# Moving the scratch writes of v from SyncE's queue to ScalarE's, with a new plan, in an RWKV block

## The chip, the cores and the metric

The kernel runs on one core of one Trainium2 chip. The metric is device time in microseconds of one execution; the time before is the median of 3 runs.

## The reference

One RWKV layer over 8 batches of 256 tokens and 512 channels, in float32, with 32 heads of 16. Cut to what matters:

```
xn = layernorm(x);  sx = shift(xn) - xn
five mixes x5[g] = xn + sx * (maa[g] + tanh((xn + sx*maa_x) @ maa_w1)[g] @ maa_w2[g])
w = exp(-exp(time_decay + tanh(x5[1] @ decay_w1) @ decay_w2))
k, v, r = x5[0] @ Wk.T, x5[2] @ Wv.T, x5[3] @ Wr.T;   g = silu(x5[4] @ Wg.T)

for each token t, per head:            # s is a 16x16 state, kept over t
    a = k_t (outer) v_t
    out_t = r_t @ (u * a + s)
    s = a + w_t * s

x = x + (groupnorm(out) * g) @ Wo.T    # time mixing
x = x + sigmoid(xr @ Wfr.T) * (square(relu(xk @ Wfk.T)) @ Wfv.T)   # xr, xk: mixes of layernorm(x)
```

The state of each head and each of its 16x16 entries is a recurrence over 256 tokens.

## The kernel before

Each batch goes through three stages. `inputs_of_scan` loads x, normalizes and transposes it (channels on partitions), makes the five mixes and projects k, v, r, g and the decay. `scan` runs the recurrence. `rest` does the group norm, the output projection Wo, and the feed-forward part with the weights fk, fr and fv, which are streamed from memory again for each batch. The stages of three batches in a row overlap: while batch b is scanned, batch b+1 is projected and batch b-1 finished.

The scan works on four blocks of 128 channels (8 heads) per batch. Partitions hold the 16 key entries of 8 heads; the value entries are spread over four steps of four. Every partition needs v of its own head, so v must be copied to other partitions. This is done through scratch tiles in memory, called vo: v of a block is written to vo (128 KB, L665), and for each of the four steps a transfer reads 32 rows of vo, repeated over the partitions, into an SBUF tile vs (512 KB, L685). ScalarE puts the state at the start into the first column of vs (L687), VectorE multiplies it with k (`kv`, L690) and runs the recurrence (`tensor_tensor_scan`, L692), GpSimd multiplies by r (L695), and TensorE adds up over the keys (`gather`, L703).

v comes out of PSUM by a ScalarE copy in `projected` (L642); one copy holds two blocks. There are 4 vo tiles, 4 vs tiles, 3 tiles of v and 3 PSUM tiles `ps` for projections. TensorE does the projections in pieces of four matmuls, by `project` (L538) and `project_tokens` (L553).

All transfers, 32 vo writes and 128 vs reads among them, are made by the helper `dma` and issued by SyncE (L366), in one queue in order.

The order of all work is set by a planner, `Plan`, that runs when the kernel is built. `Plan.add` records each operation with its engine, an estimated duration and the buffers it reads and writes. `Plan.order` then plays the work through: it keeps a time for each engine and picks the operation with the smallest sum of its earliest start and `PULL` times its rank. The ranks are the long list of integers `AIMS`, one for each operation of each stage of each batch. After an operation on another engine, one waits for `LATENCY` more:

```
    LATENCY = {"PE": 0.25, "DVE": 0.12, "ACT": 0.2, "POOL": 0.15, "DMA": 2.6}
    ...
                same = o.engine == op.engine
                o.ready = max(o.ready, op.end + (0.03 if same else self.LATENCY[op.engine]))
```

All transfers are of the engine "DMA" to the planner, so in the plan of before a vs read may follow the vo write that it needs by 0.03 us. In the running kernel it waits on a semaphore until the write has landed, and SyncE's queue with it. The order that comes out is the order of the instructions in each engine's queue.

Of the kernel before, what the change touches and what calls it, by code (L numbers as in the profile page):

```python
# [13 lines left out]
NB, T, E = 8, 256, 512  # L14
# [42 lines left out]
class Plan:  # L57
# [21 lines left out]
    def add(self, engine, us, outs, ins, emit, mode=None, into=()):  # L79
        op = Op(engine, us, outs, ins, emit, mode)  # L80


        op.bufs += [b for b in into if b not in op.bufs]
        edges = set()
        for b in ins:
            edges.add(b.writer)
            b.readers.append(op)
        for b in outs:
            edges.add(b.writer)
            edges.update(b.readers)  # L90
            b.writer, b.readers = op, []
        for o in edges - {None, op}:
            op.before.append(o)
            o.after.append(op)
        self.stages[-1].append(op)

    def stage(self):
# [116 lines left out]
    """  # L214
    PULL = 0.01

    def sequence(self, phases):
        self.ops = []
# [666 lines left out]
```

## Time and profile before

| what | value |
|---|---|
| median of 3 runs | 763.6 us (762.99 to 765.69) |
| profiled execution | 770.98 us, span 769.2 us |
| mean granted TensorE clock | 0.968 |
| TensorE busy | 692.6 us (90%) |
| VectorE busy | 596.7 us (78%) |
| GpSimd busy | 558.0 us (73%) |
| ScalarE busy | 345.6 us (45%) |
| moved by the transfers | 124.47 MB, mean 162 GB/s |
| hardware queue of SyncE | 123.84 MB, 59.4% of 16 engines' span |

In the profile's rows the engines are PE (TensorE), DVE (VectorE), ACT (ScalarE), POOL (GpSimd) and SP (SyncE); SPq is SyncE's queue of instructions, whose transfers aren't counted as busy time. A row of waits reads "who <- whom: us in total, times, longest us". The chain is the work that ended last, followed back to what released each step; its shares are of the span. A row of a stretch gives its length and, for each engine, busy time and the number of instructions, then the granted clock, the busy share of the 16 DMA engines and GB/s. A row of a transfer gives KB each and the median us from issue to landing.

### The profile page before, as it was taken

The numbers are of one execution on the slowest core, as the hardware profiler recorded it, in microseconds if no ns is written. First come the engines' busy times: TensorE is split into PE (matmuls) and PEld (weight loads), VectorE is DVE, ScalarE is ACT, GpSimd is POOL, SyncE is SP. The second block draws the span as 40 slices with busy tenths as digits, with TensorE's granted clock in tenths as the row PEclk, the third lists the DMA queues.
The fourth block names the chain that finished last, engine by engine and source line by source line (L and its number), as shares of the span: only waits on it lengthen the run. The fifth ranks groups of instructions, "written<-read, shape, count | busy, mean of one in ns | idle before, by whom it ended". The sixth has DMA issues, their size and how long they took to land.

```text
span 769.2 us, 10151 instructions
## 1 busy us (share of the span) xinstructions
PE 692.6 (90%) x3616; PEld 457.3 (59%) x3616; DVE 596.7 (78%) x612; ACT 345.6 (45%) x672; POOL 558.0 (73%) x462
## 2 busy tenths in 40 slices
PE   4897797999889998999989998999988998998987
PEld 3585465667555566657655675656755475644553
DVE  1437897999989985998689997979688988899120
ACT  4342432514673325742476334654365244534441
POOL 3546685679988777987679778788686875978351
PEclk9799799999979999999999999999998999999999
DMA  8857345364665648753759547863577628774632
GB/s 270 284 123 191 78 116 147 101 157 119 176 171 122 162 117 214 213 154 100 184 139 260 130 119 184 222 187 111 127 180 219 150 91 189 214 202 133 196 136 82
DMA packets 53889, 124.47 MB, mean 162 GB/s; under 512 B 6928, under 2 KB 12432, under 8 KB 53840
## 3 DMA queue, kind: packets, MB, share of 16 engines
q1 hardware_dynamic: 53840, 123.84, 59.4%
q8 instruction: 28, 0.46, 0.3%
q14 instruction: 21, 0.17, 0.1%
HBM read 115.43 MB, written 8.39 MB: 161 GB/s over the span
## 4 chain that ended last, share of the span: by engine, by line
PE 30%; DMA 10%; DVE 10%; issue 2%; ACT 2%; POOL 2%; SPq 1%; POOLq 0%; DVEq 0%; ACTq 0%
PE ps L553 11%; PE ps L538 9%; DMA vs<-vo 7%; DVE st L692 5%; DVE kv L690 4%; DMA vo<-v 3%; PE pat L703 2%; PE ps L592 2%; PE ps L569 2%; PE ps L612 1%; PE pat L675 1%; PE ps L738 1%; POOL mix L525 1%; SPq L366 1%; DVE mix L601 1%
## 5 line engine op out<-in xcount | busy, mean ns | idle before, releaser
L695 POOL TENSOR_TENSOR st<-st,r 128x1024 f32<-128x1024 f32 x128 | 301.5, 2357 | 79.7 <-DVE st L692 77.0
L692 DVE TENSOR_TENSOR_SCAN st<-wrep,kv 128x1024 f32<-128x1024 f32 x128 | 292.1, 2282 | 15.3 <-PE pat L703 4.4
L690 DVE TENSOR_TENSOR kv<-vs,kp 128x1024 f32<-128x1024 f32 x128 | 156.7, 1224 | 54.1 <-ACT vs L687 47.4
L687 ACT ACTIVATE vs<-s,cm 128x4 f32<-128x4 f32 x128 | 38.1, 299 | 189.4 <-DMA vs<-vo 177.1
L553 PE MATMUL ps<-Ws,mix 128*128 128x512 f32 x256 | 117.1, 598 | 6.0 <-ACT r L642 2.0
L603 POOL TENSOR_TENSOR mix<-mix,xn 128x512 f32<-128x512 f32 x80 | 86.3, 1091 | 16.1 <-DVE mix L601 15.9
L601 DVE SCALAR_TENSOR_TENSOR mix<-ps,vec,sx 128x256 f32<-128x256 f32 x160 | 67.7, 475 | 19.0 <-PE ps L592 18.5
L553 PEld LDWEIGHTS ps<-Ws,mix 128*128 128x128 f32 x256 | 47.2, 190 | 59.3 <-issue 46.5
L703 PE MATMUL pat<-st,con 128*32 128x256 f32 x1024 | 72.5, 407 | 6.0 <-POOL st L695 5.2
L538 PE MATMUL ps<-mix,Wg 128*128 128x256 f32 x256 | 62.9, 397 | 10.8 <-ACT ta L576 4.7
L538 PE MATMUL ps<-mix,Ws 128*128 128x256 f32 x256 | 60.9, 387 | 4.3 <-POOL mix L525 2.6
L538 PEld LDWEIGHTS ps<-mix,Wg 128*128 128x128 f32 x256 | 49.4, 197 | 23.5 <-ACT ta L576 5.1
L538 PE MATMUL ps<-mix,Wr 128*128 128x256 f32 x256 | 60.5, 384 | 2.2 <-ACT v L642 1.8
L553 PE MATMUL ps<-Ws,g 128*128 128x512 f32 x128 | 58.9, 599 | 2.1 <-POOL g L750 1.1
L538 PE MATMUL ps<-mix,Wv 128*128 128x256 f32 x256 | 58.7, 383 | 2.3 <-POOL mix L603 1.1
L538 PE MATMUL ps<-mix,Wk 128*128 128x256 f32 x256 | 59.5, 383 | 1.2 <-ACT r L642 0.9
L538 PEld LDWEIGHTS ps<-mix,Ws 128*128 128x128 f32 x256 | 48.0, 192 | 16.8 <-POOL mix L525 5.0
L703 PEld LDWEIGHTS pat<-st,con 128*32 128x32 f32 x1024 | 32.6, 115 | 40.6 <-issue 14.2
L525 POOL TENSOR_TENSOR mix<-mix,xn 128x512 f32<-128x512 f32 x48 | 52.1, 1092 | 5.9 <-ACT mix L523 5.9
L538 PEld LDWEIGHTS ps<-mix,Wk 128*128 128x128 f32 x256 | 47.9, 190 | 13.0 <-issue 4.0
L538 PEld LDWEIGHTS ps<-mix,Wv 128*128 128x128 f32 x256 | 47.7, 190 | 12.9 <-POOL mix L603 2.7
L538 PEld LDWEIGHTS ps<-mix,Wr 128*128 128x128 f32 x256 | 48.0, 192 | 11.5 <-ACT v L642 2.8
(77 smaller groups left out, 867.2 us busy)
## 6 DMA issues: line engine op xcount, KB each, us to landing
vs<-vo SPq DMA_DIRECT2D x128, 512.0 KB, 4.8
Ws<-in_fk SPq DMA_DIRECT2D x32, 256.0 KB, 4.3
Ws<-in_wo SPq DMA_DIRECT2D x32, 256.0 KB, 4.6
Ws<-in_fr SPq DMA_DIRECT2D x32, 256.0 KB, 4.2
Ws<-in_fv SPq DMA_DIRECT2D x32, 256.0 KB, 4.4
xt<-in_x SPq DMA_DIRECT2D x16, 256.0 KB, 4.8
x<-in_x SPq DMA_DIRECT2D x16, 256.0 KB, 4.8
vo<-v SPq DMA_DIRECT2D x32, 128.0 KB, 4.8
```

What stands on the lines that cost most here:

```text
L525: gp(512, t, [t, xn[q]], lambda q=q, t=t: nc.gpsimd.tensor_tensor(t(), t(), xn[q]()[:, :, 1 : T + 1], ALU.add), 1.8)
L538: nc.tensor.matmul(ps()[:, m, :], lhsT=w[k]()[:, o : o + P], rhs=src[k // 2]()[:, k % 2, :], start=(k == 0), stop=(k == NK - 1),)
L553: nc.tensor.matmul(ps().rearrange("p m t -> p (m t)"), lhsT=src[h]()[:, k % 2, n * P : (n + 1) * P], rhs=w[k](), start=(k == 0), stop=(k = ...
L569: nc.tensor.matmul(px()[:, i, :], lhsT=w1()[:, k, i * P : (i + 1) * P], rhs=xin[k // 2]()[:, k % 2, :], start=(k == 0), stop=(k == NK - 1),)
L592: nc.tensor.matmul(ps[g, q]()[:, m, :], lhsT=w2()[lo : lo + MAA, k * P : (k + 1) * P], rhs=ta()[lo : lo + MAA, i, :], start=True, stop=True,)
L601: dve(256, [t], [p_, vec, sx[q]], lambda g=g, q=q, m=m, t=t, p_=p_: nc.vector.scalar_tensor_tensor(t()[:, m, :], p_()[:, m, :], col(f"maa_ ...
L603: gp(512, t, [t, xn[q]], lambda q=q, t=t: nc.gpsimd.tensor_tensor(t(), t(), xn[q]()[:, :, 1 : T + 1], ALU.add), 1.8)
L687: act(4, vs, [s0, cm], lambda i=i, blk=blk, vs=vs: nc.scalar.activation(vs()[:, :, 0:1], s0()[:, blk, 4 * i : 4 * i + 4].rearrange("p (n o ...
L690: dve(4 * T, [kv], [vs, kp], lambda m=m, vs=vs, kv=kv, kp=kp: nc.vector.tensor_tensor(kv(), vs(), kp()[:, m : m + 1, :].to_broadcast([P, 4 ...
L692: dve(4 * T, [st], [w, kv], lambda w=w, kv=kv, st=st: nc.vector.tensor_tensor_scan(st().rearrange("p n t -> p (n t)"), w().rearrange("p n ...
L695: gp(4 * T, st, [st, r], lambda m=m, st=st, r=r: nc.gpsimd.tensor_tensor(st(), st(), r()[:, m : m + 1, :].to_broadcast([P, 4, T]), ALU.mult))
L703: nc.tensor.matmul(pat()[32 * i : 32 * i + 32, 0, :], lhsT=con()[:, s : s + 32], rhs=done[i]()[:, j, :], start=(j == 0), stop=(j == 3),)
```

## The change

The vo write is taken from the helper `dma` and issued by ScalarE (`nc.scalar.dma_start`), which puts it on ScalarE's own hardware queue. To the planner it is an operation of ScalarE of 0.5 us whose result is there 0.2 + 1.9 = 2.1 us after its end: `add` takes a `lag` for that, each operation carries its own `op.lag`, and the short 0.03 us between two operations of one engine holds only for those with a lag under 1, so no longer for a transfer that reads what another one wrote. All the integers of `AIMS` and `PULL` are replaced. What is computed, the tiles and the buffers stay.

```
-    def add(self, engine, us, outs, ins, emit, mode=None, into=()):
+    def add(self, engine, us, outs, ins, emit, mode=None, into=(), lag=0.0):
         op = Op(engine, us, outs, ins, emit, mode)
+        op.lag = self.LATENCY[engine] + lag
...
     AIMS = """
-        -664 -111 -501 -184 -363 -1421 -163 -60 -19 -194 201 188 -323 -12 166 -419 -366 -388 11 112 -1280
...
+        1 24 -4 17 28 45 31 38 50 16 11 52 46 38 60 67 62 63 36 47 17 51 -41 75 -17 3 7 -7 -3 20 29 56 51
...
-    PULL = 0.01
+    PULL = 0.0607
...
-                b.until = max(b.until, op.end + self.LATENCY[op.engine])
+                b.until = max(b.until, op.end + op.lag)
...
-                same = o.engine == op.engine
-                o.ready = max(o.ready, op.end + (0.03 if same else self.LATENCY[op.engine]))
+                same = o.engine == op.engine and op.lag < 1
+                o.ready = max(o.ready, op.end + (0.03 if same else op.lag))
...
             vo = new("vo", f"vo{b}_{blk}")
-            dma(vo, lambda m=m, v=v: v()[:, m, 0:T], vo, 128, v)
+            plan.add("ACT", 0.5, [vo], [v], lambda m=m, v=v, vo=vo: nc.scalar.dma_start(
+                out=vo(), in_=v()[:, m, 0:T]), lag=1.9)
```

216 rows, old and new, of the table AIMS are left out of this document.

## The prediction

> **What bounds the kernel now.** I read the page first (busy shares, chain, groups), then the waits of the two in-order queues that the change touches, then the stretch from one batch's scan to the next.
>
> ```profile
> span 769.2 us, 10151 instructions
> PE 692.6 (90%) x3616; PEld 457.3 (59%) x3616; DVE 596.7 (78%) x612; ACT 345.6 (45%) x672; POOL 558.0 (73%) x462
> ...
> PE 30%; DMA 10%; DVE 10%; issue 2%; ACT 2%; POOL 2%; SPq 1%; POOLq 0%; DVEq 0%; ACTq 0%
> PE ps L553 11%; PE ps L538 9%; DMA vs<-vo 7%; DVE st L692 5%; DVE kv L690 4%; DMA vo<-v 3%; PE pat L703 2%; PE ps L592 2%; PE ps L569 2%; PE ps L612 1%; PE pat L675 1%; PE ps L738 1%; POOL mix L525 1%; SPq L366 1%; DVE mix L601 1%
> ```
>
> TensorE is the fullest engine and has the largest part of the chain, so time is won where TensorE stands idle, and at most that much: 769.2 - 692.6 = 76.6 us. The second thing on the chain is the way of v through memory: 7% for the reads (vs from vo) and 3% for the writes (vo from v), the only part of the chain that the change names.
>
> Stretches from the first vo write of each batch to that of the next (the first eight rows; the eighth ends with the last scan, the ninth is the tail) show how full each engine is there:
>
> ```profile
> core 0: us, PE busy (x) PEld busy (x) DVE busy (x) ACT busy (x) POOL busy (x), PEclk, DMA share, GB/s
> 44.68:114.96 70.28, 60.36 (x321) 44.16 (x323) 54.41 (x53) 25.60 (x54) 45.80 (x33) 0.90 0.56 139
> 114.96:185.65 70.69, 62.99 (x374) 44.47 (x367) 64.02 (x69) 23.00 (x46) 50.27 (x36) 0.98 0.50 127
> 185.65:282.07 96.42, 88.50 (x474) 56.57 (x474) 89.65 (x84) 44.09 (x87) 78.08 (x58) 0.95 0.57 154
> 282.07:365.67 83.60, 79.13 (x433) 53.93 (x432) 69.89 (x76) 41.58 (x80) 67.94 (x62) 0.98 0.64 164
> 365.67:453.86 88.19, 82.78 (x457) 55.74 (x457) 75.80 (x75) 46.78 (x90) 70.14 (x51) 1.00 0.63 168
> 453.86:542.68 88.82, 84.24 (x455) 55.70 (x455) 77.01 (x82) 47.32 (x92) 72.94 (x64) 1.00 0.63 166
> 542.68:629.85 87.17, 80.38 (x428) 52.78 (x427) 73.50 (x71) 39.48 (x76) 67.22 (x50) 0.96 0.63 164
> 629.85:709.30 79.45, 72.04 (x365) 43.33 (x364) 69.21 (x59) 38.21 (x75) 60.53 (x43) 1.00 0.66 179
> 709.30:769.20 59.90, 52.85 (x195) 28.34 (x194) 10.77 (x17) 20.19 (x36) 22.71 (x23) 0.99 0.42 140
> sum 724.52, PE 663.28 PEld 435.03 DVE 584.26 ACT 326.26 POOL 535.63; mean PE 73.70 PEld 48.34 DVE 64.92 ACT 36.25 POOL 59.51
> ```
>
> Stretch less PE busy is TensorE's idle time: 9.9, 7.7, 7.9, 4.5, 5.4, 4.6, 6.8 and 7.4 us in the eight stretches, 54.2 together, and 7.1 in the tail. Even the tail has TensorE 88% busy, with work of the batch before still in it. So an idle microsecond saved in the eight stretches should come off the end nearly one for one.
>
> Now the queue of SyncE, which issues every transfer in order, and the engines behind it:
>
> ```profile
> SPq L366 <- DVE kv L690: 215.0, 74, 7.5
> SPq L366 <- DMA vo<-v: 75.7, 19, 9.0
> SPq L366 <- PE ps L553: 64.6, 33, 11.0
> SPq L366 <- ACT v L642: 59.7, 11, 12.6
> SPq L366 <- DMA vs<-vo: 50.6, 17, 6.4
> ```
> ```profile
> ACT vs L687 <- DMA vs<-vo: 177.1, 81, 8.4
> ...
> DVE kv L690 <- ACT vs L687: 47.4, 19, 11.8
> ```
>
> 215.0 us of SyncE's waiting is harmless: it waits for a vs tile to come free. 59.7 us is waiting for v to be computed before a vo write, and 75.7 us for a vo write to land before its first vs read; all other transfers queue behind. ScalarE's column write into vs (L687) then waits 177.1 us for the reads, and VectorE 47.4 us for that write. The start of a batch, here the last one, looks like this on SyncE's queue:
>
> ```profile
> 629.85 0.33 SPq L366 DMA_DIRECT2D vo<-v  x1
> 631.63 2.45 SPq L366 DMA_DIRECT2D vs<-vo  x4
> 634.41 0.33 SPq L366 DMA_DIRECT2D vo<-v  x1
> 643.86 1.16 SPq L366 DMA_DIRECT2D vs<-vo  x2
> 645.11 0.54 SPq L366 DMA_DIRECT2D vo<-v  x1
> ```
> ```profile
> vs<-vo SPq DMA_DIRECT2D x128, 512.0 KB, 4.8
> ...
> vo<-v SPq DMA_DIRECT2D x32, 128.0 KB, 4.8
> ```
> ```profile
> 629.85 1.70 DMA vo<-v
> 634.41 9.30 DMA vo<-v
> ```
>
> The first write lands in 1.70 us, with nothing before it. The second is issued behind four reads of 512 KB and takes 9.30 us for 128 KB, and the reads of its block go out at 643.86, just after. A small write stands behind large reads; this is what a queue of its own takes away.
>
> **The change, part by part.** (1) 32 vo writes leave SyncE's queue for ScalarE's. On SyncE one takes 0.33 (the rows above) to 0.59 us; I take 0.43, so 32 x 0.43 = 13.7 us more on ScalarE, whose 345.6 us busy become some 359 of 769. I cost it at nothing: its cover is ScalarE's 423 us of idle time; if that cover is gone it costs up to 13.7. The bound below is zero, as the instruction does no work there that another removes.
>
> (2) A write's waits move with it. v is made by ScalarE's own copy (L642), so the 59.7 us of SyncE standing for v go, and the weights, x rows and reads behind it are issued earlier. The other wait comes along: a vo buffer (four of them) must have been read by its four vs reads of the batch before. Behind a ScalarE that waits stand the copies out of PSUM (L642), for which TensorE waits, the vs columns (L687), for which VectorE waits, and the decay expansion (L670). That is the price of the slower rival below.
>
> (3) Landing of the writes. Where no reads stand ahead it is 1.70 us, now in the median 4.8. The 19 waits of SyncE cost 75.7 us, 4.0 each; at 1.7 each they would be 32, so some 43 us of queue time go. That isn't time on the path; its worth is read from the engines around the starts of batches. The sum over seven such windows (110 to 140, 180 to 215, 278 to 308, 365 to 392, 450 to 486, 540 to 572 and 628 to 664 us):
>
> ```profile
> sum 226.00, PE 200.56 PEld 146.31 DVE 177.32 ACT 110.49 POOL 170.04; mean PE 28.65 PEld 20.90 DVE 25.33 ACT 15.78 POOL 24.29
> ```
>
> TensorE idles 226.0 - 200.6 = 25.4 us there, 11.3%. In the remaining 438.6 us of the eight stretches it idles 28.8, or 6.6%; at that rate the windows would hold 14.8, so the excess is 10.6 us. VectorE has 48.7 us idle in the windows against 9.7% elsewhere: an excess of 26.8. The first count is what is lost if TensorE's other work goes on as now, the second what the scan could come forward.
>
> The first batch is apart, since nothing of a batch before can fill TensorE. Between 44 and 72 us SyncE waits
>
> ```profile
> SPq L366 <- DMA vo<-v: 18.1, 4, 8.4
> SPq L366 <- ACT v L642: 11.9, 2, 11.7
> ```
>
> and this stretch has the most idle time of the eight, 9.9 us against 4.5 in the best: another 5.4.
>
> (4) The new plan. All numbers of AIMS and the weight PULL are replaced, so the order on every engine and on SyncE's queue changes. The plan before let a vs read follow its vo write by 0.03 us, while the profile shows 1.7 at best; now it counts 2.1 after the issue, so it can put other transfers between them. What the rest of the new order does is in no row. Bounds: all eight stretches with no idle time (-54.2 us), or all with as much as the worst, 9.9 (8 x 9.9 = 79.2, so +25). I take the best stretch, 4.5 us, for all eight: 54.2 - 8 x 4.5 = 18 us saved. It is nearest to the two counts above, 10.6 + 5.4 = 16.0 from TensorE, and below VectorE's 26.8.
>
> What is late next is TensorE itself: 79 to 84 us busy in a stretch of 84 to 89; after it VectorE with 70 to 77. So there is no second large gain behind the first.
>
> **The sum.** The profiled execution took 770.98 us (769.2 of span and 1.8 around it), 1.0% over the median of 763.6. 770.98 - 18 = 753.0; times 763.6 / 770.98 that is 745.8; I say 746, 2.3% less.
>
> **The rivals.** *More is won*: the scans come forward by the 27 us that VectorE shows and the filler moves up, so that TensorE's idle time halves again to 2.25 a stretch: 54.2 - 18 = 36 saved, 728 us. For it: the idle rows of VectorE. Against: TensorE would be 97% busy throughout, and no stretch is over 95% now.
>
> *Nothing is won.* If the second queue doesn't shorten the landings, because the transfers share the same engines that are 50 to 66% busy in the stretches, only SyncE's 13.7 us of issuing move, and SyncE isn't the bound: 764 us. Against it stands the first pair of rows, 1.70 us alone and 9.30 behind reads.
>
> This is a rule of the Trainium skill: DMA: Bandwidth & Descriptors, section "Issuing engines are not separate DMA queues", says that transfers run on the same 16 DMA engines whoever starts them, and that issuing from several saves only the issuing time. The same page, "Queues, rings and completion order", says that a DMA engine takes turns between queue rows packet by packet, by which a small write of another row would not wait for four whole reads; the 9.30 us row fits that, but no run yet shows a second queue.
>
> *Slower: ScalarE stands for vo buffers.* Blocks 2 and 3 of a batch are copied together, while the scan of the batch before may still read its last vo buffers. If each of these two writes stops ScalarE for the longest wait that SyncE shows for vs reads, 6.4 us, and two pieces of projection that TensorE can still put in PSUM cover 2 x 1.73 = 3.46 of it,
>
> ```profile
> 317.75 1.73 PE ps L538 x8
> ```
>
> then 2.9 us are open, twice in seven batches: 41 us, less the 18 won, +23, or 786 us. It decides from 18 / 14 = 1.3 us open per write. For it: ScalarE already stops 81 times for reads. Against: the plan knows the buffers and the landings, and four buffers are a whole batch. *A poorer order* (all stretches like the worst, +25, 789) is the tail of the same side.
>
> **How the numbers follow.** Forecast 0.52 (735 to 760, at 746), more won 0.16, nothing won 0.13 (760 to 767), ScalarE stopped 0.13, poorer order 0.06. Changes within 0.5%, 3.8 us, can't be told from none. Faster is 0.52 + 0.16 = 0.68, same 0.13, slower 0.19. The range 724 to 770 holds the forecast, nothing won, most of more won and the least of the slower cases; about 0.04 lies below and 0.16 above.
>
> **What would show it.** Right: a second hardware queue with 32 x 128 KB; vo landing near 2 us in the median; SyncE's waits for ACT v gone and for vo well under 75.7; the chain's two DMA shares under 10% together; TensorE's idle time in the middle about 36 us. Wrong: vo landing still 4.8 or more; ScalarE's queue waiting for vs reads ahead of vo writes; TensorE waiting for ScalarE's copies; or busy time of TensorE growing with a lower granted clock, so that fewer idle microseconds bring nothing.

## The result, and the profile after

| | before | changed |
|---|---|---|
| median, 4 runs each | 764.6 us | 739.8 us (734.4 to 744.7) |
| ratio, 95% interval | | 0.966 (0.958 to 0.975) |
| profiled execution | 770.98 us | 741.01 us |

The change takes 24.8 us off the median; 18 had been forecast. Four executions of the experiments below were slow ones (748.1 us in run 1, 770.6 in run 2, 1170.1 in run 5, 3893.6 in run 11): they stand in the medians but not in the ratios, and the profile of run 5 is of its slow one, so no row of it is shown.

The page of the changed kernel, its busy shares, its chain and its queues of transfers (q10 is the new one, ScalarE's: 4.20 MB of writes that q1 no longer carries):

```profile
span 739.2 us, 10182 instructions
PE 681.0 (92%) x3616; PEld 457.3 (62%) x3616; DVE 596.4 (81%) x612; ACT 335.8 (45%) x664; POOL 558.3 (76%) x462
...
q1 hardware_dynamic: 49232, 119.64, 60.1%
q10 hardware_dynamic: 4608, 4.20, 1.9%
...
PE 48%; DVE 15%; DMA 9%; POOL 6%; ACT 4%; issue 2%; POOLq 0%; SPq 0%; DVEq 0%; ACTq 0%
PE ps L537 21%; PE ps L552 14%; DMA vs<-vo 8%; DVE st L692 7%; PE pat L703 5%; DVE kv L690 4%; POOL st L695 4%; PE ps L591 3%; PE ps L568 1%; DVE mix L600 1%; POOL mix L524 1%; PE ps L611 1%; PE pat L675 1%; PE ps L738 1%; POOL sx L511 1%
```

The shares of a chain add up to the part of the span over which it could be followed, 57% before and 84% now. So TensorE's 30% and 48% are 53% and 57% of what was followed, and the transfers' 10% and 9% are 18% and 11% of it. The vo writes, 3% before, are no longer among the lines shown; the vs reads are at 8%, 7% before. The stretches between the first vo writes of the batches, as before, again with the tail last:

```profile
42.62:106.31 63.69, 59.62 (x327) 47.20 (x327) 53.66 (x54) 25.57 (x52) 45.55 (x33) 0.95 0.62 150
106.31:177.07 70.76, 64.19 (x377) 44.52 (x377) 66.97 (x67) 27.61 (x51) 51.06 (x38) 0.93 0.50 133
177.07:264.80 87.73, 81.75 (x468) 54.05 (x467) 83.30 (x82) 43.97 (x88) 74.92 (x56) 0.98 0.59 159
264.80:350.58 85.78, 81.25 (x447) 54.65 (x447) 80.08 (x81) 42.27 (x84) 75.03 (x63) 1.00 0.67 173
350.58:442.56 91.98, 91.23 (x490) 62.10 (x490) 77.68 (x84) 50.32 (x101) 76.88 (x64) 1.00 0.67 187
442.56:518.91 76.35, 75.45 (x417) 50.14 (x419) 62.30 (x65) 34.45 (x69) 58.83 (x51) 1.00 0.64 162
518.91:598.90 79.99, 75.09 (x431) 51.11 (x421) 74.00 (x69) 35.31 (x70) 66.88 (x44) 0.98 0.64 165
598.90:677.48 78.58, 72.31 (x369) 43.70 (x369) 74.92 (x67) 39.32 (x79) 64.69 (x51) 1.00 0.74 201
677.48:739.20 61.72, 52.05 (x184) 27.58 (x182) 9.93 (x15) 20.07 (x36) 21.09 (x22) 0.95 0.37 119
sum 696.58, PE 652.96 PEld 435.04 DVE 582.84 ACT 318.88 POOL 534.94; mean PE 72.55 PEld 48.34 DVE 64.76 ACT 35.43 POOL 59.44
```

In the eight stretches TensorE is idle for 634.9 - 600.9 = 34.0 us, 54.2 before: 20.2 less. Its busy time there also fell, from 610.4 to 600.9: 9.5 less. The first write comes 2.1 us earlier, and the tail is 1.8 us longer. Together that is the 30.0 us between the two spans. This pair of profiled executions lies further apart than the medians: the one before is 6.3 us over its median, the changed one 1.2.

The waits of SyncE's queue and the chain of waits behind the vs reads, in the changed kernel:

```profile
SPq L365 <- DVE kv L690: 277.1, 88, 7.3
SPq L365 <- DMA vo<-v: 56.4, 11, 15.1
```
```profile
ACT vs L687 <- DMA vs<-vo: 137.5, 79, 5.2
...
DVE kv L690 <- ACT vs L687: 11.1, 6, 4.6
```
```profile
vo<-v ACTq DMA_DIRECT2D x32, 128.0 KB, 3.6
```

VectorE waits 11.1 us for a filled vs tile where it waited 47.4, and the writes land in 3.6 us instead of 4.8. This looks like the forecast coming true. The experiments show that it came true for another reason than the one with which the prediction began.

### The profile page after: what moved, and what is told of

Same layout as the page of the kernel before. It is cut to its first block, busy times and chain, and to the rows that moved or that the text cites. A ratio compares the mean times of both kernels' runs of the same rounds, so it can differ in the third digit from the quotient of the medians.

```text
span 739.2 us, 10182 instructions
## 1 busy us (share of the span) xinstructions
PE 681.0 (92%) x3616; PEld 457.3 (62%) x3616; DVE 596.4 (81%) x612; ACT 335.8 (45%) x664; POOL 558.3 (76%) x462
## 4 chain that ended last, share of the span: by engine, by line
PE 48%; DVE 15%; DMA 9%; POOL 6%; ACT 4%; issue 2%; POOLq 0%; SPq 0%; DVEq 0%; ACTq 0%
PE ps L537 21%; PE ps L552 14%; DMA vs<-vo 8%; DVE st L692 7%; PE pat L703 5%; DVE kv L690 4%; POOL st L695 4%; PE ps L591 3%; PE ps L568 1%; DVE mix L600 1%; POOL mix L524 1%; PE ps L611 1%; PE pat L675 1%; PE ps L738 1%; POOL sx L511 1%
## 5 line engine op out<-in xcount | busy, mean ns | idle before, releaser
L690 DVE TENSOR_TENSOR kv<-vs,kp 128x1024 f32<-128x1024 f32 x128 | 156.6, 1223 | 14.3 <-ACT vs L687 11.1
L602 POOL TENSOR_TENSOR mix<-mix,xn 128x512 f32<-128x512 f32 x80 | 86.2, 1093 | 13.9 <-DVE mix L600 13.9
L703 PE MATMUL pat<-st,con 128*32 128x256 f32 x1024 | 67.4, 396 | 4.0 <-POOL st L695 3.0
L537 PE MATMUL ps<-mix,Wv 128*128 128x256 f32 x256 | 61.8, 389 | 2.3 <-POOL mix L602 2.3
L537 PE MATMUL ps<-mix,Wk 128*128 128x256 f32 x256 | 62.2, 391 | 0.9 <-DVE att L745 0.9
L537 PE MATMUL ps<-mix,Wg 128*128 128x256 f32 x256 | 58.0, 381 | 0.0
L537 PEld LDWEIGHTS ps<-mix,Wv 128*128 128x128 f32 x256 | 49.2, 195 | 11.1 <-POOL mix L602 3.2
```

The costliest lines, as they stand in the source:

```text
L537: nc.tensor.matmul(ps()[:, m, :], lhsT=w[k]()[:, o : o + P], rhs=src[k // 2]()[:, k % 2, :], start=(k == 0), stop=(k == NK - 1),)
L602: gp(512, t, [t, xn[q]], lambda q=q, t=t: nc.gpsimd.tensor_tensor(t(), t(), xn[q]()[:, :, 1 : T + 1], ALU.add), 1.8)
L690: dve(4 * T, [kv], [vs, kp], lambda m=m, vs=vs, kv=kv, kp=kp: nc.vector.tensor_tensor(kv(), vs(), kp()[:, m : m + 1, :].to_broadcast([P, 4 ...
L703: nc.tensor.matmul(pat()[32 * i : 32 * i + 32, 0, :], lhsT=con()[:, s : s + 32], rhs=done[i]()[:, j, :], start=(j == 0), stop=(j == 3),)
```

## The experiments

**Two theories.** *Own queue*: the writes no longer stand behind the large reads, land sooner, and SyncE no longer stands for v. *Plan*: the old order was laid out by a planner that let a read follow its write at once; the chip had to wait for the landing, and everything arranged around it came late. The new order has the landing in it. A third reading, *quality*, is that the new ranks are simply better. The planner works out a span of its own when the kernel is built (`self.span`): 731.5 us for the kernel before and 728.4 for the changed one. The two plans are 3 us apart, the two kernels 25; so quality by the planner's own measure isn't the difference.

**1. The new order, but the old queue.** The plan is untouched; only the emitted instruction is another:

```
-            plan.add("ACT", 0.5, [vo], [v], ... nc.scalar.dma_start(
+            plan.add("ACT", 0.5, [vo], [v], ... nc.sync.dma_start(
```

> The changed kernel with its whole plan, order and positions, but each write of vo is issued by SyncE at that place instead of by ScalarE. Own-queue theory (the second queue's shorter landing brings most of the 25 us): 755 us or more, SyncE again waits some 60 us for v copies. Plan theory (the new order brings most): 740 to 748 us, as the order already leaves room for the landing.

Measured: 741.7 us, 0.966 of before (0.962 to 0.970), the same as the changed kernel. SyncE's waits in it, and the landing of the writes:

```profile
SPq L664 <- ACT v L641: 42.9, 10, 14.3
...
SPq L365 <- DMA vo<-v: 15.1, 8, 4.0
```
```profile
vo<-v SPq DMA_DIRECT2D x32, 128.0 KB, 3.2
```

SyncE stands 42.9 us for v again, and no cost of it can be told from the noise. The writes land in 3.2 us on the shared queue: so the order alone makes them land sooner, too. The last batch shows how. Before, one write was followed by four reads, then the second write, which took 9.30 us. Here both writes of a v copy go out together, ahead of the reads (SyncE's queue, this run):

```profile
601.33 0.81 SPq L664 DMA_DIRECT2D vo<-v  x2
603.09 2.73 SPq L365 DMA_DIRECT2D vs<-vo  x2
```

**2. The old order, but the new queue.**

```
-            dma(vo, lambda m=m, v=v: v()[:, m, 0:T], vo, 128, v)
+            plan.add("DMA", 0.05 + 128 / 300, [vo], [v], ... nc.scalar.dma_start(out=vo(), in_=v()[:, m, 0:T]))
```

> The kernel before with its plan, ranks and order, but each write of vo is issued by ScalarE at the place the old plan gives it. Own-queue theory: 752 us or less, the median landing of vo near 3.6 us, SyncE's waits for v copies gone. Plan theory: 758 to 768 us, since the order of the reads and of the engines is the old one.

Measured: 764.7 us, ratio 0.997 (0.995 to 1.000). Its landing and its waits:

```profile
vo<-v ACTq DMA_DIRECT2D x32, 128.0 KB, 3.3
```
```profile
SPq L366 <- DMA vo<-v: 136.8, 17, 16.7
```

The own queue does shorten the landing, 4.8 to 3.3 us, and is worth some 2 us, at most 4 by the interval. SyncE's 136.8 us are the two waits of before added up, 75.7 + 59.7 = 135.4: the reads behind the write need v all the same, so the wait for v has only changed its name. The own-queue theory falls with these two runs.

**3 and 4. Ranks and planner crossed.** In the third run the kernel before gets only the new `AIMS` and `PULL`, in the fourth the changed kernel gets the old ones.

> The kernel before with only the new AIMS and PULL: vo writes on SyncE, and a plan that lets a read follow its write by 0.03 us. Own-queue theory: 762 to 768 us. Plan theory in the form that the ranks do it: 740 to 750 us. Plan theory in the form that knowing the landing does it: 755 us or more.

> The changed kernel (own queue, landing in the plan) with only the old AIMS and PULL. Own-queue theory: 738 to 750 us. Plan theory by the ranks: 760 us or more, as the old ranks were made for another plan. Plan theory by the landing: 740 to 752 us.

Measured: 855.4 us (ratio 1.117, 1.113 to 1.121) and 906.1 us (1.180, 1.175 to 1.184). The two expectations that hold these numbers are open at the top and belong to opposite forms of the plan theory; neither meant so much. The new ranks bring nothing by themselves: the planners make 827.7 and 887.1 us of them in their own reckoning. Each set fits its own planner only, and these two runs can't tell what knowing the landing is worth.

**5 and 6. No landing to wait for.** The order is kept and the write is made, but the read takes its bytes from an input:

```
-  dma(vs, lambda i=i, vo=vo: vo()[32 * i : 32 * i + 32] ...
+  dma(vs, lambda i=i, vo=vo: x[0, 0:64, :].rearrange("r (a t) -> (r a) t", a=2)[32 * i : 32 * i + 32] ...
```

> The kernel before with its order, but the vs reads take the same number of bytes from the input x instead of from vo, so no read waits for a write to land; the vo writes are still made, and the output isn't the reference's. The old plan puts its own span at 731.5 us with no landing between write and read, the new one its own at 728.4 with it. Accuracy theory (the old order is as good as the new one but for the landing that its plan left out): 738 to 748 us. Quality theory (the new order is better in itself): 755 us or more.

> The changed kernel with its order, and the vs reads taken from the input x as in the run before, so without the wait for the landing; the output isn't the reference's. Accuracy theory: 734 to 740 us, since the plan has the landing hidden already. If the waits for vo that SyncE still shows (56 us) are on the path: 725 us or less.

Measured: the kernel before goes to 734.6 us (ratio 0.960, 0.958 to 0.963), the changed kernel to 737.7 (0.965, 0.960 to 0.970; with the wait it is 0.966). Without the landing the two orders differ by no more than their intervals. So the old order lost 30 us to the landing, more than expected, and the new one loses none that can be measured: the 56.4 us that SyncE still waits for vo aren't on the path. Run 6 is also the control for the edit, which changes two more things. The bytes come from another place: the reads land in 4.7 us in run 6 and in 4.8 in the changed kernel, and its time hardly moves. And a vo write no longer has to wait until its buffer has been read. That wait was not taken away alone; in run 1, where the vo writes have a line of their own, it is small:

```profile
SPq L664 <- DMA vs<-vo: 8.3, 3, 3.8
```

**7. The ranks with a plan moved a little.** `lag=1.9` becomes `lag=2.0`.

> The changed kernel with a lag of 2.0 instead of 1.9 us in the plan and the same ranks. The plan puts its own span at 768.1 us instead of 728.4. If the ranks are a fit to one exact plan, the chip follows: 772 to 785 us. If they carry a good order by themselves: 738 to 748 us.

Measured: 775.9 us, ratio 1.015 (1.012 to 1.018). A tenth of a microsecond in one estimate makes the plan 768.1 us, and the chip follows. The given ranks are a fit to one exact planner.

**8 to 11. Four planners, each with ranks of its own.** To compare planners and not leftover ranks, each gets a search of its own with the same start and the same effort. In these kernels `AIMS` and `PULL` are replaced by what the search found, and the rest is as the expectation says (for the eleventh, `add` and `order` are those of the change and the write stays a `dma`).

> The kernel before (vo on SyncE, the old plan without the landing), with ranks searched anew: started from the start times in the changed kernel's plan, PULL 1, 40 minutes of random changes judged by the plan's own span, which ends at 724.8 us, lower than both given plans. Accuracy theory: 750 to 762 us, as before some 30 us over its plan. Quality theory (new ranks of the kind are better): 735 to 742 us.

> The changed kernel (vo on ScalarE, lag 1.9), ranks searched from the same start with the same effort; the plan's own span is 723.8 us. Accuracy theory: 733 to 739 us, some 11 over the plan. Quality theory: 735 to 742 us as well; the pair with the search under the old plan tells the two apart.

> The changed kernel with a lag of 3.4 instead of 1.9 us, which makes the landing in the plan 3.6 us as the trace of the changed kernel shows, ranks searched from the same start with the same effort; the plan's own span is 729.4 us. If the rest between plan and chip is the landing too: 732 to 737 us. If it is something else (clock, matmul ends): 739 to 743 us, 11 over the plan.

> vo writes left to SyncE's queue, as before, but a plan that waits 2.6 us for their landing, ranks searched from the same start with the same effort; the plan's own span is 727.2 us. If the queue doesn't matter and the landing in the plan does: 736 to 742 us. If ScalarE's queue matters after all: 748 us or more.

Measured: 748.1 us for the old planner (ratio 0.977, 0.974 to 0.981), 726.0 for the new one (0.948, 0.944 to 0.952), 727.0 with the lag of 3.4 (0.949, 0.946 to 0.952), and 729.8 with the landing in the plan and the writes on SyncE (0.953, 0.949 to 0.957). All four are lower than the accuracy theory had said, which had taken the distance between plan and chip over from the given ranks, 30 us for the old planner and 11 for the new. The order among them is the one it said, with the old planner alone at the far end, but for the lag of 3.4, which gained nothing over 1.9. Their waits for a filled vs tile, old planner and new planner (lines are shifted: L602 is the column write, L605 the multiplication by k in the first, L604 and L607 in the second):

```profile
ACT vs L602 <- DMA vs<-vo: 178.0, 65, 8.0
...
DVE kv L605 <- ACT vs L602: 31.9, 12, 7.0
```
```profile
ACT vs L604 <- DMA vs<-vo: 141.2, 61, 5.5
...
DVE kv L607 <- ACT vs L604: 14.4, 9, 5.7
```

**12. The old planner's new order, with no landing to wait for.** The edit of runs 5 and 6 on run 8.

> The kernel with ranks searched under the old plan, same order, but the vs reads taken from the input x, so that no read waits for a vo write to land; the output isn't the reference's. Accuracy theory: the 23 us between its plan (724.8) and the chip (748.1) are the landing, so 725 to 730 us. If the old plan's order is poorer in another way too: 735 us or more.

Measured: 728.8 us (ratio 0.953, 0.950 to 0.956). VectorE's wait falls with it:

```profile
DVE kv L605 <- ACT vs L602: 17.0, 6, 5.9
```

What the plans said and what the chip took, side by side:

| kernel | landing in the plan | plan's own span | chip, median | difference |
|---|---|---|---|---|
| before | no | 731.5 | 764.6 | +33.1 |
| before, writes on ScalarE (2) | no | 731.5 | 764.7 | +33.2 |
| before, reads don't wait (5) | no, and none on the chip | 731.5 | 734.6 | +3.1 |
| changed | yes | 728.4 | 739.8 | +11.4 |
| changed, writes on SyncE (1) | yes | 728.4 | 741.7 | +13.3 |
| changed, reads don't wait (6) | yes, but none on the chip | 728.4 | 737.7 | +9.3 |
| before with the new ranks (3) | no | 827.7 | 855.4 | +27.7 |
| changed with the old ranks (4) | yes | 887.1 | 906.1 | +19.0 |
| changed, lag 2.0 (7) | yes | 768.1 | 775.9 | +7.8 |
| searched, old planner (8) | no | 724.8 | 748.1 | +23.3 |
| the same, reads don't wait (12) | no, and none on the chip | 724.8 | 728.8 | +4.0 |
| searched, new planner (9) | yes | 723.8 | 726.0 | +2.2 |
| searched, landing in the plan, SyncE (11) | yes | 727.2 | 729.8 | +2.6 |
| searched, lag 3.4 (10) | yes | 729.4 | 727.0 | -2.4 |

With searched ranks, plans within 1 us of each other (runs 8 and 9) are 22 us apart on the chip, and taking the wait away from the slower one brings it to within 3 us. So the landing that the plan left out is shown to be the cause, at 19 us in run 8's order and 30 in that of the kernel before. It isn't all that a plan can lack: run 4 has the landing in its plan and is 19.0 us over it. Run 9 also shows a second gain, some 14 us (739.8 to 726.0) with the same planner and queue: the plans are 4.6 us apart, so most of that is an order that carries over to the chip better. Why the changed kernel's ranks lie 9 to 13 us over their plan, and the searched ones with the landing in the plan within 3 us of theirs, wasn't settled. The version of run 9 beats both kernels.

## Why the prediction was right or wrong

**Bound and account: right; the size in part luck.** Time came off where TensorE stood idle: the prediction expected 36 us of idle time left in the eight stretches, and 34.0 are left. Busy time wasn't in the sum and gave 9.5 us more there in the profiled pair, which is most of what the forecast was short by. That the idle time came so near is partly luck. The 4.5 us of the best stretch followed from no mechanism, and no even 4.5 came of it: the stretches now idle between 0.8 and 6.6 us. Two of them have TensorE 99% busy, though the prediction held it against *More is won* that none was over 95%. And the 16.0 us that stood behind the 18 were counted for the queue, which is worth some 2 us.

**Step 1, issuing on ScalarE costs nothing: right.** With the same order, writes on ScalarE and on SyncE take 739.8 and 741.7 us. The 359 us of busy time that it expected on ScalarE can't be read there, since the profile counts no issuing as busy: the row went from 345.6 to 335.8. An issue took SyncE up to 0.88 us, not 0.59; its median of 0.43 is as read.

**Step 2, SyncE freed from standing for v: wrong.** It was true of the row and of no worth: run 2 has the same total under one name, and run 1 keeps 42.9 us of it at no cost that shows. In run 2 the reads behind the write wait for it in SyncE's place.

**Step 3, the landing on a queue of its own: the step that failed.** The row of 1.70 us against 9.30 was read as the effect of sharing a queue, and 10.6 + 5.4 us were given to it. Run 2 measures it as 0.3% (0 to 0.5%), run 1 as nothing that can be told. The signs that the prediction set came out in between: the writes land in 3.6 us, neither near 2 nor still 4.8, and SyncE waits 56.4 us for them, not well under 75.7. The time around batch starts was there to be had: in the 32 us behind the first vo write of batches 2 to 8 TensorE idles 25.4 us before and 13.7 in the changed kernel, 11.7 less where 10.6 had been counted, and the first stretch idles 4.1 us instead of 9.9, where 5.4 had been counted. But the new order brought it and not the queue. By the rule of the Trainium skill named in the prediction (DMA: Bandwidth & Descriptors, "Issuing engines are not separate DMA queues") little was to be won by another queue; the times of runs 1 and 2 agree with it, while the landing of 3.3 us in run 2 against 4.8 shows that the queue isn't without effect.

**Step 4, the new plan: the right mechanism, named and not weighed.** The prediction saw that the plan counted 0.03 us where the chip needed at least 1.7, and yet took its size from idle time, as a rest. The price came out when the wait was taken away: 30 us in run 5.

**The rivals.** "Nothing won" was right about the queue and wrong about the time, since it forgot the plan. ScalarE stopping for vo buffers didn't decide anything: run 2, with ScalarE's writes in an order that knew nothing of it, isn't slower. For a poorer order +25 us was set as the end; runs 3, 4 and 7 show +91, +141 and +11 from ranks that don't fit their planner, so that bound was far too narrow for such a mismatch.

## What to carry to other kernels

Where an order is made by a planner, compare its span with the chip before anything else: this plan was 33 us short, and taking one wait away on the chip, with the order unchanged, showed that 30 of them were that wait. Correct the planner's model first and search the order again under it, since ranks fitted to another planner, even to one 0.1 us away in one estimate, made the kernel slower than before here (runs 3, 4 and 7). A wait that is long in the table of a queue is no price: in run 2 the writes left for another queue, and SyncE's total and the time stayed where they were.

## What the runs showed of the hardware that was not expected

TensorE's busy time isn't fixed by the work. Over the thirteen profiled executions with a mean granted clock of 0.897 to 0.984, all with the same 3616 matmuls, it went from 673.8 us at 0.984 (run 10) to 734.1 at 0.897 (run 4), and busy time times clock stays between 658 and 670 us. The three with the most idle time have the lowest clock (171 us idle at 0.897 in run 4, 129 at 0.926 in run 3, 82 at 0.948 in run 7), so idle time may be paid partly twice, as itself and as slower matmuls; that was not tried by itself.
